# A decoder kernel on one core: expert rows beyond 256 in pieces of 128, and two value products elsewhere

## The chip, the core and the metric

The kernel runs on one NeuronCore of a Trainium2 chip. Its engines have queues of their own and work in order, each: TensorE (PE) multiplies matrices from SBUF into PSUM, VectorE (DVE), ScalarE (ACT) and GpSimd (POOL) work elementwise, SyncE (SP) issues transfers. ACT and POOL issue transfers too; those through a list of row numbers (indirect ones) are issued by POOL. The metric is the device time in microseconds; lower is better. All data is float32, and a float32 matmul stands in the profile as two matmuls and two weight loads.

## The reference, cut to what matters

Two decoder layers follow one another on x, of shape 4 x 512 x 256, each sublayer with a residual and a layer norm. The third one is a mixture of experts: each of the 2048 rows goes to two of 8 experts.

```python
x = layernorm(x + L0_attn(x))               # a recurrence per token
x = layernorm(x + L0_xattn(x, ctx, ctx))    # one head, 1601 context rows
# experts: top 2 of softmax(x @ Wr + br), weights made to sum to 1
h = gelu(xf @ Wi[e] + bi[e]) * sigmoid(xf @ Wg[e] + bg[e])    # 256 -> 1024
r = xf + (h @ Wo[e] + bo[e])
y = (r - mean(r)) * rsqrt(var(r) + 1e-12) * gamma[e] + beta[e]
x = layernorm(x + sum_of_two(weight * y))
x = layernorm(x + L1_attn(x))               # 16 heads, causal
x = layernorm(x + L1_xattn(x, ctx, ctx))    # 16 heads, rotated queries and keys
x = layernorm(x + L1_ffn(x))
```

The number of rows that an expert gets depends on the data, so the kernel must be right for any split of 4096 rows over 8 experts.

## The kernel before, in words

Each stage handles the four batches in turn. In the stages of this study the order of instructions on every engine is the order of the program (`manual_schedule`); waits are put in by the framework, from the tiles that an instruction reads and writes.

**Cross attention of the first layer and routing** (from line 608). For 16 tiles of 128 queries: scores, exponentials, transposed and weighted sums. When a batch is through, the generator `closing` (L719) goes through its tail in steps, one step between the pieces of other work: normalise, transpose x (`to_xT`, L195), then `route` (L457): router logits, softmax, the two largest, ranks by a matmul with a triangular matrix (`before`, `both`), and a row number for each of the row's two places. `scatter` (L528) writes the rows of the batch with 8 indirect transfers into the DRAM array `xs`, 2048 row places per expert. The last batch's tail has no other work beside it. Then `blocks_left` (L539) makes the list of the further blocks.

**Experts** (from line 821). Expert e's first 256 rows are block e. Rows beyond are in further blocks of 256: at most NDYN = 15 of them can be needed, and all 15 are run, so there are 8 + 15 = 23 blocks. Which expert and which rows a further block has stands in `wrow` and `xrow`; its weights and rows come by indirect transfers on POOL's queue, those of the first 8 by plain ones on SP's. The loop (L1007 to L1016) keeps two blocks under way: `begin` loads rows and weights (two buffers for each of eWi, eWg, eWo), `turned` transposes the rows, `first_half` makes the two products with 1024 columns and gelu, sigmoid and their product g, `second_half` the product back to 256, residual, moments, gamma and beta, and stores to the DRAM array `ys`. PE works on block i's first half, then on block i-1's second half. Beside this, the generator `attention_first` (L914) prepares the attention, one step per block.

**Attention of the second layer** (from line 1026). First the sums of the experts' results are gathered back (`combined`, L1069), keys and values of the context are made (`context`, L1173: `key` with a rotation, `value`), then 32 units (batch, group of 4 heads, self or cross) run, the units of cross attention last. The lists `extras` hold work that is put between a unit's pieces; among it are the keys and values of batches 2 and 3 (`later`, L1613), loaded in chunks of the context (`cx`).

Of the kernel before, what the change touches and what calls it, by code (L numbers as in the profile page):

```python
# [17 lines left out]
P = 128  # L18
# [21 lines left out]
def decoder(ctx: ExitStack, tc: tile.TileContext, a: dict, out: bass.AP):  # L40
# [166 lines left out]


    with (
# [55 lines left out]
        xs = tc.dram_tile((ROWS, D), F32, name="xs")  # L265

        def clear_rows():
            zero = p1w.tile([P, 1024], F32, tag="zero", name="zero")
            nc.gpsimd.memset(zero, 0.0)
            zrows = xs.rearrange("(n p r) d -> n p (r d)", p=P, r=4)  # L270
            for i in range(ROWS // (4 * P)):
                nc.sync.dma_start(zrows[i], zero)

# [111 lines left out]
    BLK = 2 * P  # L385
    NDYN = 2 * B * S // BLK - 1
    ys = tc.dram_tile(((E + NDYN) * BLK, D), F32, name="ys")

# [28 lines left out]
    for name, n in (("iota", E), ("base", E), ("more", E - 1), ("upto", E * E), ("dyn", NDYN), ("p", 2)):  # L417
        fields[name] = cmoe[:, at_ : at_ + n]
        at_ += n
# [119 lines left out]
    def blocks_left():  # L539
# [5 lines left out]
        more = prt.tile([P, E, E - 1], F32, tag="more", name="more")  # L545
        nc.vector.tensor_tensor(
            more,
            n[:, :, None].to_broadcast([P, E, E - 1]),
            fields["more"][:, None, :].to_broadcast([P, E, E - 1]),
# [4 lines left out]
        upto = prt.tile([P, E, E], F32, tag="upto", name="upto")  # L554
# [8 lines left out]
        past = prt.tile([P, NDYN, E], F32, tag="past", name="past")  # L563
# [12 lines left out]
        nc.vector.tensor_scalar(j, j, 1.0, float(E - 1), ALU.add, ALU.min)  # L576
# [4 lines left out]
        nc.vector.tensor_scalar(xf, j, float(BLK), None, ALU.mult)  # L581
# [5 lines left out]
        xrow = prt.tile([P, 2, NDYN], I32, tag="xrow", name="xrow")  # L587
        for h in range(2):
            nc.vector.tensor_scalar(xrow[:, h, :], xf, fields["p"][:, h : h + 1], None, ALU.add)
# [6 lines left out]
        nc.vector.tensor_tensor(yf, yf, eks, ALU.subtract)  # L596
# [8 lines left out]
        return wrow, xrow  # L605


    with tc.tile_pool(name="p2", bufs=2) as p2, ExitStack() as ordered:
# [135 lines left out]

        def tail():
            if tails and next(tails[0], tails) is tails:
                tails.pop(0)
# [21 lines left out]
        while tails:  # L769
            tail()  # L770
        ordered.close()
        scatter(B - 1, lambda inst: unordered("xs", inst))
        wrow, xrow = blocks_left()
# [8 lines left out]
    VW = HD + 1  # L782
# [38 lines left out]
    with tc.tile_pool(name="p3", bufs=2) as p3, ExitStack() as ordered:  # L821
# [8 lines left out]
        def begin(i):  # L830

            e = i if i < E else wrow[:, i - E : i - E + 1]
            xb = p3.tile([P, 2, D], F32, tag="xb", name="xb", bufs=3)
            if i < E:
                nc.sync.dma_start(
                    xb, xs[i * B * S : i * B * S + BLK, :].rearrange("(h p) d -> p h d", p=P)
                )
            else:
                for h in range(2):
                    nc.gpsimd.indirect_dma_start(  # L840
                        xb[:, h, :],
                        None,
                        xs,
                        bass.IndirectOffsetOnAxis(ap=xrow[:, h, i - E : i - E + 1], axis=0),
                    )
            wi, wg = expert_first[i] if i < 2 else load_expert(e, expert_in, pmw)
            return i, e, wi, wg, xb

        def turned(i, e, wi, wg, xb):
# [9 lines left out]
            return i, e, wi, wg, xb, xbT  # L859

        def first_half(i, e, wi, wg, xb, xbT):

            (wo,) = load_expert(e, ("eWo",), p3)
            g = p3.tile([P, NF, BLK], F32, tag="g", name="g")
            for w, func in ((wi, AF.Gelu), (wg, AF.Sigmoid)):
                for f0 in range(0, NF, 4):
                    ps = wide()
                    pv = ps.rearrange("p a (h n) -> p (a h) n", n=BLK)
                    dst = g[:, f0 : f0 + 4, :]
                    if w is wg:  # L870
                        dst = p3.tile([P, 4, BLK], F32, tag="sg", name="sg")
                    for k in range(4):
                        f = f0 + k
# [3 lines left out]
                                (w[:, c * FF + f * P : c * FF + (f + 1) * P], xbT[:, c, :])  # L877
# [3 lines left out]
                    for k in range(4):  # L881
                        bias = w[:, 2 * FF + f0 + k : 2 * FF + f0 + k + 1]
                        nc.scalar.activation(dst[:, k, :], pv[:, k, :], func, bias=bias)  # L883
                    if w is wg:
                        part = g[:, f0 : f0 + 4, :]
                        nc.vector.tensor_tensor(part, part, dst, ALU.mult)  # L886

            bo = wo[:, None, NF * D : NF * D + D].to_broadcast([P, 2, D])
            nc.gpsimd.tensor_tensor(xb, xb, bo, ALU.add)
            return i, wo, xb, g  # L890

        def second_half(i, wo, xb, g):
            ps = bank()
            pv = ps.rearrange("p (h d) -> p h d", d=D)
            for h in range(2):
                blk = slice(h * P, (h + 1) * P)
                mm(pv[:, h, :], [(g[:, f, blk], wo[:, f * D : (f + 1) * D]) for f in range(NF)])
            r = p3.tile([P, 2, D], F32, tag="rb", name="rb")
            nc.vector.tensor_tensor(r, pv, xb, ALU.add)
            mv = moments(r, 2)  # L900
            rs = rstd_of(mv, eps12, 2)
            for h in range(2):
                nc.vector.tensor_scalar(
                    r[:, h, :], r[:, h, :], mv[:, h, 0:1], rs[:, h : h + 1], ALU.subtract, ALU.mult
                )
            gam, bet = (
                wo[:, None, (NF + k) * D : (NF + k + 1) * D].to_broadcast([P, 2, D]) for k in (1, 2)
            )
            eng = nc.vector if i == E + NDYN - 1 else nc.gpsimd
# [944 lines left out]
```

## Time and profile before

| | us |
|---|---|
| median of three runs (2436.15 to 2438.79) | 2437.68 |
| the profiled execution | 2439.88 |
| its span | 2438.0 |
| PE busy | 2344.4 |
| DVE busy | 1211.7 |
| ACT busy | 1073.5 |
| POOL busy | 422.7 |
| first matmul of the first expert block | 524.86 |
| end of the last expert block on PE | 1023.1 |
| first self-attention unit ends | 1129.6 |
| cross units | 1488 to 2314 |

A group's line has the program line, the engine, the operation, the tiles (out<-in) with their shapes, the count, and behind the bar the busy time, the mean length of one in ns, and the idle time of the engine just before, with what ended it. Matmuls overlap one another, so the mean length is more than their spacing. In a timeline a line has start, length, and the idle time before it in brackets. L202 is the helper `mm`, through which most matmuls go: the tiles tell them apart.

### The profile page before, as it was taken

Reading aid. Unit: us, or ns where it says so; the run is one execution under the profiler, and the core shown is the slowest. Engines: PE = TensorE matmul, PEld = TensorE weight load, DVE = VectorE, ACT = ScalarE, POOL = GpSimd, SP = SyncE. Lnnn points to the kernel's source line nnn. Section 1 sums busy time; section 2 is a strip of 40 time slices with the busy share of each in tenths; the row PEclk is TensorE's granted clock in tenths of the full one; section 3 lists DMA queues with packets and bytes.
Section 4 is the critical chain, followed back from the end, with each engine's and each line's share of the span. In section 5 each row is a group of like instructions: output and inputs, shape, how many; then the busy total and the mean of one; then the engine's idle time right before and its main releaser. Section 6 shows DMA issues by size and latency. Waiting matters only on the chain.

```text
span 2438.0 us, 34867 instructions
## 1 busy us (share of the span) xinstructions
PE 2344.4 (96%) x13928; PEld 1328.2 (54%) x13928; DVE 1211.7 (50%) x2854; ACT 1073.5 (44%) x1996; POOL 422.7 (17%) x429
## 2 busy tenths in 40 slices
PE   7898999959999999989999999999999999999998
PEld 4767677748888888843333334333333333333256
DVE  1333334322222233266656667666666666677334
ACT  1111122114444544424555453655666566566730
POOL 1010001121144433345130010222110010000000
PEclk9999999969999999989999997999999999999999
DMA  8300311145667555351211210112110110100100
GB/s 307 150 1 3 124 54 45 49 143 186 247 239 266 198 204 201 124 164 50 66 48 35 95 36 5 39 51 60 51 37 16 45 36 16 30 34 18 31 9 26
DMA packets 76112, 215.84 MB, mean 89 GB/s; under 512 B 11816, under 2 KB 35630, under 8 KB 66862
## 3 DMA queue, kind: packets, MB, share of 16 engines
q1 hardware_dynamic: 61790, 133.04, 16.1%
q0 software_dynamic: 10992, 65.54, 7.3%
q10 hardware_dynamic: 3168, 15.03, 1.8%
q8 instruction: 110, 1.80, 0.3%
q14 instruction: 52, 0.43, 0.1%
HBM read 171.53 MB, written 53.21 MB: 92 GB/s over the span
## 4 chain that ended last, share of the span: by engine, by line
PE 51%; ACT 1%; DVE 1%; issue 0%; DVEq 0%; ACTq 0%
PE s L1310 23%; PE one L202 12%; PE po L1337 11%; PE s L202 2%; PE s L1320 1%; PE one L1295 1%; PE one L1358 1%; ACT x L171 0%; ACT ex L1324 0%; DVE one L1269 0%; PE one L1379 0%; PE one L1477 0%; PE one L1400 0%; DVE pm L1267 0%; DVE st L156 0%
## 5 line engine op out<-in xcount | busy, mean ns | idle before, releaser
L1324 ACT ACTIVATE ex<-s 128x512 f32<-128x512 f32 (+1 forms) x1062 | 577.9, 594 | 466.9 <-PE s L1310 236.7
L1267 DVE TENSOR_REDUCE pm<-one 128x1 f32<-128x512 f32 x768 | 493.7, 685 | 174.5 <-PE s L1310 123.3
L1310 PE MATMUL s<-q,kc 32*128 32x512 f32 x1612 | 524.1, 640 | 0.2 <-ACT ex L1324 0.2
L202 PE MATMUL one<-kc,qt 32*128 32x512 f32 (+1 forms) x2048 | 483.8, 564 | 0.3 <-DVE pm L1267 0.3
L1310 PEld LDWEIGHTS s<-q,kc 32*128 32x128 f32 x1612 | 161.6, 179 | 210.9 <-issue 175.5
L1337 PE MATMUL po<-ex,v 128*32 128x256 f32 (+3 forms) x2472 | 245.1, 465 | 0.3 <-ACT ot L1350 0.3
L1269 DVE CUSTOM_DVE_ANT_0 one<-one,c_diagq 128x512 f32<-128x512 f32 x256 | 171.9, 716 | 75.6 <-PE one L202 63.5
L1310 PE MATMUL s<-q,ks 32*128 32x512 f32 x512 | 179.8, 650 | 5.3 <-ACT ex L1324 4.9
L1337 PEld LDWEIGHTS po<-ex,v 128*32 128x32 f32 (+1 forms) x2472 | 49.8, 108 | 232.2 <-issue 225.5
L886 DVE TENSOR_TENSOR g<-g,sg 128x1024 f32<-128x1024 f32 x46 | 57.2, 1243 | 235.8 <-ACT sg L883 235.7
L202 PE MATMUL wide<-xbT,eWi 128*128 128x256 f32 x736 | 168.9, 389 | 4.0 <-DVE xbT L858 4.0
L202 PEld LDWEIGHTS one<-kc,qt 32*128 32x128 f32 x2048 | 164.2, 188 | 11.6 <-DVE pm L1267 7.9
L202 PE MATMUL wide<-xbT,eWg 128*128 128x256 f32 x736 | 162.6, 379 | 0.0
L202 PE MATMUL bank<-eWo,g 128*128 128x256 f32 x736 | 162.5, 379 | 0.0
L202 PEld LDWEIGHTS wide<-xbT,eWi 128*128 128x128 f32 x736 | 143.5, 196 | 25.8 <-issue 4.2
L202 PE MATMUL one<-ks,qt 32*128 32x512 f32 x512 | 152.6, 665 | 3.7 <-ACT raw L1182 2.7
L202 PEld LDWEIGHTS wide<-xbT,eWg 128*128 128x128 f32 x736 | 139.7, 190 | 19.2 <-ACT g L883 0.2
L1150 POOL TENSOR_TENSOR raw<-raw,c_cos 128x512 f32<-128x512 f32 (+1 forms) x32 | 34.9, 1092 | 660.5 <-DVE swp L1149 578.1
L202 PEld LDWEIGHTS bank<-eWo,g 128*128 128x128 f32 x736 | 138.2, 190 | 17.9
L883 ACT ACTIVATE g<-wide,eWi 128x256 f32<-128x256 f32 x184 | 71.7, 476 | 72.3 <-PE wide L202 69.7
L1310 PEld LDWEIGHTS s<-q,ks 32*128 32x128 f32 x512 | 53.8, 185 | 83.4 <-issue 62.0
L202 PE MATMUL wide<-ctxT,q 128*128 128x512 f32 (+1 forms) x256 | 91.3, 510 | 0.8 <-DVE q L649 0.8
(319 smaller groups left out, 2988.4 us busy)
## 6 DMA issues: line engine op xcount, KB each, us to landing
xs<-zero SPq DMA_DIRECT2D x32, 512.0 KB
kc<-kcd SPq DMA_DIRECT2D x16, 800.5 KB
eWo<-in_eWo SPq DMA_DIRECT2D x8, 1408.0 KB
cx<-in_ctxT SPq DMA_DIRECT2D x18, 512.0 KB
eWi<-in_eWi SPq DMA_DIRECT2D x8, 1028.0 KB
eWg<-in_eWg SPq DMA_DIRECT2D x8, 1028.0 KB
qt<-qd SPq DMA_DIRECT2D x32, 256.0 KB
ctxT<-in_ctxT SPq DMA_DIRECT2D x4, 1601.0 KB
```

The source lines that it names most:

```text
L202: nc.tensor.matmul(ps, l, r, start=(i == 0), stop=(i == n - 1))
L883: nc.scalar.activation(dst[:, k, :], pv[:, k, :], func, bias=bias)
L886: nc.vector.tensor_tensor(part, part, dst, ALU.mult)
L1150: eng.tensor_tensor(raw[:, :n], raw[:, :n], cos[:, :n], ALU.mult)
L1267: nc.vector.tensor_reduce(pm[:, t, j, c : c + 1], ps, AX.X, ALU.max)
L1269: nc.vector.tensor_tensor_reduce(out=ps, in0=ps, in1=diagq[:, 384 - t * P : 896 - t * P], scale=1.0, scalar=LOWEST, op0=ALU.add, op1=ALU.m ...
L1295: nc.tensor.transpose(pt[:, t * P : (t + 1) * P], ng.rearrange("p j r -> p (j r)"), ident)
L1310: nc.tensor.matmul(ps[:kn], kt[rows, k * P : k * P + kn], q2[rows, :], start=True, stop=cross)
L1320: nc.tensor.matmul(ps[:, k * P : (k + 1) * P], later_[:, :P], later_[:, P:], start=False, stop=True)
L1324: nc.scalar.activation(ex[:kn, h, :], ps[:kn], AF.Exp)
L1337: nc.tensor.matmul(state["po"][j * 32 : j * 32 + 32, q0:q1], (vals if cross else vself)[b % 2][:kn, k, c0 : c0 + 32], ex[:kn, j % 2, q0:q1 ...
L1358: nc.tensor.transpose(pt[:, t * P : (t + 1) * P], ot[:, t * P : (t + 1) * P], ident)
```

## The change

The further rows of an expert go in pieces of 128 rows instead of blocks of 256. A block takes two pieces, each with its own expert, so a block of pieces needs two sets of weights, and its first products have 128 columns instead of 256. At most NDYN = 28 pieces can be needed, 14 blocks. Eleven of them run always, mixed with the 8 first ones in the order `ffmfmfmmfmfmmfmfmmm` (f a first block, m one of pieces); each of the last three runs only if the list is that long, inside nested `tc.If` on a count that every engine loads into a register. Parts of `ys` that those three would write are cleared at the start. Weights are now loaded name by name and piece by piece, right after the piece of the running block that frees the buffer; the bias of the second product moves from POOL's addition on xb to a DVE addition on r, and moments and normalisation of a block of pieces are made for each half.

The values of batches 2 and 3 for the second layer's cross attention are made in the tail of the routing of the last batch: four ahead of its transposes, twelve ahead of the ranks' matmul, ten after `blocks_left`; they go to the DRAM arrays `vd` and are loaded back in one transfer each in the cross units of batches 1 and 2. DVE clears and sets the rest of these tiles. `blocks_left` now stands ahead of the last scatter.

In the start of the attention, the rotation of every second chunk of keys goes from DVE to POOL, the order of the work is changed, and the load of the exponential table stands later.

```diff
@@ clear_rows
+            for n in range(22, NDYN, 2):
+                row = E * BLK + n * P
+                nc.sync.dma_start(
+                    ys[row : row + 2 * P, :].rearrange("(p r) d -> p (r d)", r=2), zero[:, : 2 * D]
+                )
...
+        def rows_of_values():
+            big = p2in.tile([P, NT * S2], F32, tag="fs", name="v23")
+            rest = p2in.tile([P, KHALF * D], F32, tag="ctxa", name="v2")
...
+            for b_ in (2, 3):
+                nc.vector.memset(places[b_, NKT - 1], 0.0)
+            for t in (big[:, : 22 * VROW], rest[:, : 4 * VROW]):
+                t = t.rearrange("p (k r) -> p k r", r=VROW)
+                nc.vector.memset(t[:, :, NH * VW :], 0.0)
+                heads = t[:, :, : NH * VW].rearrange("p k (h r) -> p k h r", r=VW)
+                nc.vector.memset(heads[:, :, :, HD : HD + 1], 1.0)
+
+        def value(b, k):
+            kn = kn_of(k)
+            ps = bank()[:, :D]
+            mm(ps[:kn], [(ctxTs[b][:, c, k * P : k * P + kn], xaV[:, c, :]) for c in range(2)])
+            dst = places[b, k][:kn, : NH * VW].rearrange("p (h r) -> p h r", r=VW)
+            nc.scalar.copy(dst[:, :, :HD], ps[:kn].rearrange("p (h r) -> p h r", r=HD))
...
-        while tails:
-            tail()
+        values = [lambda b=b, k=k: value(b, k) for b in (2, 3) for k in range(NKT)]
+        for n in (0, 4, 0, 0, 0, 12, 0, 0, 0, 0, 0):
+            if n == 4:
+                tail()
+                rows_of_values()
+            else:
+                tail()
+            for f in values[:n]:
+                f()
+            values = values[n:]
+        assert not tails
+        wrow, xrow, count = blocks_left()
+        for f in values:
+            f()
         ordered.close()
         scatter(B - 1, lambda inst: unordered("xs", inst))
-        wrow, xrow = blocks_left()
...
+        def halves(kind, m):
+            return (m,) if kind == "first" else (2 * m, 2 * m + 1)
+
+        def weights_of(block, name, h):
+            kind, m = block
+            hs = halves(*block)
+            if h < len(hs):
+                e = m if kind == "first" else wrow[:, hs[h] : hs[h] + 1]
+                loaded.setdefault((block, name), []).extend(
+                    load_expert(e, (name,), p3 if name == "eWo" else pmw)
+                )
...
+        def first_half(block, nxt):
+            xbT = loaded.pop((block, "xT"))
             g = p3.tile([P, NF, BLK], F32, tag="g", name="g")
+            for name, func in (("eWi", AF.Gelu), ("eWg", AF.Sigmoid)):
+                ws = loaded.pop((block, name))
+                for i in range(2):
+                    if len(ws) == 1:
+                        w, fs_, cols = ws[0], range(4 * i, 4 * i + 4), slice(0, BLK)
+                    else:
+                        w, fs_, cols = ws[i], range(NF), slice(i * P, (i + 1) * P)
...
+                    if nxt and (nxt, name) not in first_loads:
+                        weights_of(nxt, name, i)
...
+        def second_half(block, nxt, after):
...
             for h in range(2):
+                wo = wos[h % len(wos)]
                 blk = slice(h * P, (h + 1) * P)
                 mm(pv[:, h, :], [(g[:, f, blk], wo[:, f * D : (f + 1) * D]) for f in range(NF)])
+                if len(wos) == 1 and h == 0:
+                    continue
+                hs = slice(0 if len(wos) == 1 else h, h + 1)
+                k = hs.stop - hs.start
+                nc.vector.tensor_tensor(r[:, hs], pv[:, hs], xb[:, hs], ALU.add)
...
+                nc.vector.tensor_tensor(r[:, hs], r[:, hs], bo, ALU.add)
...
+                eng = nc.gpsimd if nxt else nc.vector
+                eng.tensor_tensor(r[:, hs], r[:, hs], gam, ALU.mult)
+                eng.tensor_tensor(r[:, hs], r[:, hs], bet, ALU.add)
...
+                for half in range(2) if len(wos) == 1 else (h,):
+                    if nxt:
+                        weights_of(nxt, "eWo", half)
+            if after:
+                rows_of(after)
...
+        def run(blocks, work):
+            get = lambda i: blocks[i] if i < len(blocks) else None
+            for b in blocks[:2]:
+                rows_of(b)
+            for name in ("eWi", "eWg", "eWo"):
+                for h in range(2):
+                    if (blocks[0], name) not in first_loads:
+                        weights_of(blocks[0], name, h)
+            turned(blocks[0])
+            for i, b in enumerate(blocks):
+                first_half(b, get(i + 1))
+                if get(i + 1):
+                    turned(get(i + 1))
+                if i:
+                    second_half(blocks[i - 1], b, get(i + 2))
+                elif get(2):
+                    rows_of(get(2))
+                next(work, None)
+            second_half(blocks[-1], None, None)
+
+        order = "ffmfmfmmfmfmmfmfmm" + "m" * 1
...
+        def beside():
+            ready["total"] = nc.values_load(count[0:1, 0:1], min_val=0, max_val=NDYN)
+            yield from attention_first()
...
+        def rest(m):
+            if m < NDYN // 2:
+                with tc.If(ready["total"] > 2 * m):
+                    with tc.manual_schedule():
+                        run([("more", m)], iter(()))
+                    rest(m + 1)
+        rest(11)
...
-                eng = nc.gpsimd if here is None else nc.vector
+                eng = nc.gpsimd if here is None or i % 2 else nc.vector
...
-        for f in keys0[0:2] + values1 + add + keys0[4:6] + turn:
+        for f in keys0[0:2] + values1[:8] + add + values1[8:] + turn + keys0[4:6]:
...
-        later = [
-            context(2, range(4), ()) + context(3, range(2), ()),
-            context(3, range(2, 4), ()) + context(2, (), range(4)),
-            context(3, (), range(4)),
-        ]
+        later = [context(2, range(4), ()), context(3, range(4), ())]
+        for b in (2, 3):
+            starts[index[b - 1, 1, True]].append(
+                lambda b=b: nc.sync.dma_start(vals[b % 2].rearrange("p k r -> p (k r)"), vd[b])
+            )
```

## The prediction

> **What bounds the kernel now.** I read the page's slices first, then the groups, then the timeline of single engines at the two borders of the expert stage.
>
> ```profile
> span 2438.0 us, 34867 instructions
> PE 2344.4 (96%) x13928; PEld 1328.2 (54%) x13928; DVE 1211.7 (50%) x2854; ACT 1073.5 (44%) x1996; POOL 422.7 (17%) x429
> ...
> PE   7898999959999999989999999999999999999998
> ...
> DMA  8300311145667555351211210112110110100100
> ...
> L202 PE MATMUL wide<-xbT,eWi 128*128 128x256 f32 x736 | 168.9, 389 | 4.0 <-DVE xbT L858 4.0
> ```
>
> A slice is 61 us. TensorE (PE) has one hole, the slice that begins at 488 us (digit 5), where the routing of the last batch ends. The expert blocks follow (to 1023 us, PE full, DMA at 5 to 7 tenths), then the attention, again PE. The span is 2438.0, the profiled run 2439.88, the median of runs 2437.68: what lies round the span is 2 us, so I carry differences of the span straight to the median.
>
> In the timelines, a line gives start, length, instructions, and the idle time before it:
>
> ```profile
> 59.35 1.06 PE L202 MATMUL bank<-inv,dg 128*128 128x128 f32 x8
> ...
> 490.37 2.30 PE L188 MATMUL wide<-ident,x 128*128 128x128 f32 x8 [3.19 <-DVE x L726]
> ...
> 505.49 0.64 PE L202 MATMUL bank<-both,before 128*128 128x32 f32 x2 [5.75 <-DVE both L492]
> ...
> 522.99 1.09 PE L854 MATMUL bank<-ident,xb 128*128 128x128 f32 x4 [15.80 <-DMA xb<-xs]
> 524.86 10.09 PE L202 MATMUL wide<-xbT,eWi 128*128 128x256 f32 x32 [0.78 <-DVE xbT L858]
> ...
> 753.12 7.07 PE L202 MATMUL bank<-eWo,g 128*128 128x256 f32 x32
> ...
> 1024.00 7.14 PE L202 MATMUL one<-xaV,qt 128*128 128x256 f32 x32 [0.93 <-DVE rb L899]
> ```
>
> Spacing of matmuls: 32 of 256 columns take 7.07, the last of them 0.38, so (7.07-0.38)/31 = 0.216 us each. Eight of 128 columns take 1.06, the last 0.28: 0.112 each. So half the columns cost half, although each needs new weights. A block now is 96 x 0.216 + 4 transposes x 0.11 = 21.2 us, and the stores of the blocks do stand 21.2 apart. The weights' transfers are hidden:
>
> ```profile
> 747.54 0.95 POOL L397 DMA_INDIRECT eWi<-in_eWi,wrow  x1 [0.30 <-issue]
> ...
> 760.71 1.27 POOL L889 TENSOR_TENSOR xb<-xb,eWo 128x512 f32<-128x512 f32 x1 [9.70 <-DMA eWo<-in_eWo,wrow]
> ```
>
> Three transfers (3.55 MB) land 13.2 us after the first issue, in a period of 21.2.
>
> **The change, part by part.**
>
> *Blocks.* 23 blocks become 19: 8 first ones, 11 of two pieces. The last three run only for a list over 22 pieces. From the reference on its inputs I counted the rows per expert: 520, 304, 1112, 352, 989, 298, 70, 451. Beyond 256 that is 3+1+7+1+6+1+0+2 = 21 pieces, so they don't run. A block of pieces: 128 matmuls x 0.112 + 32 x 0.216 + 0.44 = 21.7. Stage: 23 x 21.2 = 487 now; 8 x 21.2 + 11 x 21.7 = 408 then: -79.
>
> Two things give back. (a) The two halves of the second product lie in one PSUM bank, and by the order of instructions the second half's first matmul now waits for the VectorE (DVE) addition of the first half. That addition stands on DVE behind the last product g (1.23) and the copy xbT (0.68), and g behind ScalarE's (ACT) last sigmoid, some 2.6 us after PE's last matmul of the first half (8 of 128 columns, 0.32 each, estimated from 1.57 for four of 256 and 1.09 for two of 512). So the addition ends near 14.3+2.8+1.2+0.7+0.4 = 19.4 in the block, PE could go on at 18.2: about 1.3 us when the block running is one of pieces (5 times with the end), 0.7 when it is a first block (6 times): +11. (b) Traffic: a block of pieces loads 7.1 MB, with rows and results 7.6. At the full rate seen (273 GB/s at a DMA share of 0.75, so 364) that is 20.9 us, under the 23 of such a block; at the pace of the lines above (3.55 MB in 13.2, latency and all) 28. Several transfers stand queued at once here, so I take the nearer first one and +4 for four places where blocks of pieces meet; ends 0 and +55. All eight indirect transfers of a block go through POOL's queue, 1.26 us each, 10 us, with 3 us of gamma and beta: under 23. Each weight load waits in that queue for PE and ACT to free its buffer; behind it stand gamma, beta and the row gathers, of which the rows have least room, some 2 us. SP's queue has the same waits for first blocks, with the ys stores behind them. The bias addition that moves from POOL to DVE (0.69) is hidden: DVE is a quarter busy. Blocks: -64.
>
> *Values of batches 2 and 3.* 26 products of 4 matmuls leave the attention. There PE is 100% busy between 1977 and 2286 us, so their time counts: 104 x 0.216 = -22.5. From one copy of the attention's sums (ACT L1350) to the next, the first three cross units of batch 2, with 40 of these matmuls, last 160.3 in all and those of batch 3, with none, 149.8; less two query projections of 1.7 that is 0.18 each, -18; the group's busy time (40.1/144 = 0.28) gives -29. I take -23. The 10 us of ACT copies were hidden; the two loads of 1.9 MB on SP's queue run at a DMA share of 0.1.
>
> They go into the hole, which is not wholly free, for the chain there passes through PE's queue. Four stand ahead of the transposes (L188), and two PSUM buffers force the third to wait for an ACT copy, which waits for new DVE memsets (about 1.9 us, six of 60 to 350 columns at the pace of the row 0.69 for 512), which wait for normalising. Transposes then start near 495.5 instead of 490.4: +5. Twelve stand ahead of "both": 48 x 0.216 = 10.4, some cold, against 5.75 idle: +6. Routing ends 11 later, then come the unchanged 8 scatters and the row load. The last ten values run under those. I give back 1 for a warmer clock: +10, ends +3 and +16.
>
> *The clock rule.* The line at 524.86 is the row: after 15.8 idle, 32 matmuls took 10.09, not 7.07: 3.0 lost. The Trainium skill (TensorE: Matmul & The Clock Gate, Part 1) says PE halves its clock after an idle window of 3.4 us and needs about as long busy to get it back, which would make 1.7 lost per hole. By the row a hole costs 3.0. This speaks against the new stop at the branch.
>
> *The branch.* Today PE idles 0.93 between stages. Now PE's first matmul after the join waits for DVE and ACT to have passed the branch, so DVE's whole tail shows. The last block's tail today is 1023.16 to 1027.61, 4.45 us, at 512 columns; at 256, with one addition more and the output bias after it, 4. Then compare, semaphores and branch: 0.5 to 1. The Trainium skill (Runtime: NRT & Kernel Launch, Instruction fetch mechanics) says that a taken branch to code outside the prefetched pages stops the engine for a fetch. The trace has no branch; a 16 KB instruction packet takes 0.94 in it. By that rule up to two fetches on the slowest engine, an estimated 2.6 each (0.94, and the 1.65 from a weight transfer's issue to its first packet); without, 0. The three skipped blocks are short (44 instructions on ACT, 25 on DVE each), so I take 1. With 4+1+1-0.9 and 3.0 cold: +8, ends +3 and +18. Later things (gathers of ys, cx loads) wait as long, and shift with it. The register loads of the count, a form not in the trace: the same page has about 0.2 us for one and 1.3 for several, so 0 to 1.5, taken 0.5 on PE.
>
> *Order after the stage.* Rotations of chunks 1 and 3 go from DVE to POOL; 0.69 x 3 becomes 1.27 x 3, behind the gathers of batch 1, which hold POOL to about 50 us after the stage. DVE gains 7 us where PE idles 2.73 and 0.98: -2, ends -6 and +4. The moved table load (1.28) is hidden on ACT. Zeroing 0.75 MB of ys more is hidden in a slice with DMA 0 to 3.
>
> **Sum.** -64 -23 +10 +8 +0.5 -2 = -70.5: 2437.7 - 70.5 = 2367 us.
>
> **Rivals.**
> 1. Likeliest, as above: 2367, own range 2345 to 2388. Chance 0.62.
> 2. DMA becomes the bound in part: each block of pieces lasts 27 us, not 23: 11 x 4 = +44: 2411. For it: 13.2 us per 3.55 MB from POOL; against it 273 GB/s without a full queue. Chance 0.16.
> 3. The hole is freer and the values dearer than I take: hole +3, values -29, branch +4: 2350, and no DMA loss: 2346. For it: PE idles 30 us there. Chance 0.14.
> 4. Slower: the indirect transfers of two experts at a time don't reach the rate. The gain of 70 is gone when a block of pieces lasts 23 + 70/11 = 29.4, that is 7.6 MB at 259 GB/s; at 245 it is 31 and the kernel 2455. The pace of the lines above, 269, is close to it. Chance 0.07.
> That the skipped blocks run (21 pieces against a bound of 22) or that nothing changes I give 0.01.
>
> **Numbers.** Runs of this kernel tell 0.2% (5 us) from no change. Ends: case 3 with the order after the stage at -6 and the branch at +3 gives 2341, so 2340 below; case 2 in full gives 2411, cut to 2405, since what lies above 2405 (half of case 2, case 4) and below 2340 should hold 2 in 10. Faster 0.92 (cases 1 to 3), same 0.01, slower 0.07.
>
> **What would show it.** Right: matmuls of 128 columns spaced 0.112; ys stores of blocks of pieces 22 to 24 apart; a PE wait of the second eWo half on DVE L991; PE idle of 5 to 8 ahead of the first xaV matmul after the branch; first block starting near 533; units of cross 1 and 2 two to four us shorter. Wrong: PE waits on DMA eWo, eWi or xb of many us in the blocks, PE clock below 1.0 there, or a POOL queue held by a buffer not yet free.

## The result, and the profile after

| | before | changed kernel |
|---|---|---|
| median | 2437.14 us | 2429.2 us (2422.99 to 2432.43) |
| ratio of the changed kernel to before, 95% interval | 1 | 0.9967 (0.9956 to 0.9977) |
| the profiled execution, its span | 2439.88, 2438.0 | 2425.35, 2423.5 |

The change gains 8 us where 70 were forecast; 2429 lies outside the range of 2345 to 2388. A second comparison on another chip, further down, gives 0.9985, with an interval that reaches 1.

The page of the changed kernel, with the same rows as before (slices of 61 us, then the groups):

```profile
span 2423.5 us, 36202 instructions
PE 2289.2 (94%) x14448; PEld 1296.1 (53%) x14448; DVE 1197.9 (49%) x2846; ACT 1063.4 (44%) x2103; POOL 435.3 (18%) x455
...
PE   7898999979898999789999999999999999999998
...
DMA  8300211145788767432210220111120010100100
...
L202 PE MATMUL bank<-eWo,g 128*128 128x256 f32 x608 | 151.9, 410 | 17.1 <-DMA eWo<-in_eWo,wrow 11.3
```

PE lost 55 us of work, but its share of the span fell from 96% to 94%: holes came in. Those in the expert blocks are seen in the slices that begin at 606, 727 and 970 us, with 8, 8 and 7 where PE had 9 before (the last of them also covers the border to the next stage). Over the blocks PE's mean granted clock went from 0.99 to 0.95. The DMA row there was at 5 to 7 tenths and is at 6 to 8.

To see how much each stretch gave, I cut both profiled executions at five marks: on PE the first expert matmul, the start of the last eWo matmul and the first xaV matmul of the next stage; on ACT the copies of the sums (ot<-po) that end the first unit and the last.

| stretch, us | before | after | difference | forecast |
|---|---|---|---|---|
| to the first expert matmul | 524.9 | 531.2 | +6.3 | +10 |
| expert blocks | 497.8 | 477.0 | -20.8 | -64 |
| border to the next stage | 1.3 | 8.0 | +6.7 | +8 (with cold PE) |
| from there to the first unit | 105.6 | 115.2 | +9.6 | -2 |
| the units | 1184.2 | 1167.9 | -16.3 | -23 |

The sum is -14.5, the difference of the two spans. Some 5 of it are chance: the router's matmuls of the batch before the last, which the change doesn't touch, began at 456.19 in this execution and at 461.24 in that of before. From there to the first expert matmul it is 63.6 before and 75.0 after: the values cost +11.4 there. Without that chance the sum is -9, near the medians.

The routing of the last batch, in the timeline of PE:

```profile
488.55 3.52 PE L202 MATMUL bank<-xaV,ctxT 128*128 128x256 f32 x8 [4.68 <-ACT v L789]
...
499.18 13.65 PE L202 MATMUL bank<-xaV,ctxT 128*128 128x256 f32 x48
512.66 0.30 PE L202 MATMUL bank<-both,before 128*128 128x32 f32 x2
...
529.34 1.09 PE L933 MATMUL bank<-ident,xb 128*128 128x128 f32 x4 [6.60 <-DMA xb<-xs]
531.21 9.54 PE L202 MATMUL wide<-xbT,eWi 128*128 128x256 f32 x32 [0.78 <-DVE xbT L937]
```

Both stops that the forecast named are there: the wait for an ACT copy of a value, and 48 matmuls that `both` waits behind.

The expert blocks show what was not forecast. First the PE waits of the stage (in total, times, longest), then a first block and what follows it in the timeline of PE:

```profile
PE bank L933 <- DMA xb<-xs,xrow: 24.0, 7, 5.8
PE bank L202 <- DMA eWo<-in_eWo,wrow: 11.3, 4, 6.9
...
PE bank L202 <- DVE rb L991: 5.2, 9, 0.6
```

```profile
595.61 7.07 PE L202 MATMUL wide<-xbT,eWi 128*128 128x256 f32 x32
602.51 7.07 PE L202 MATMUL wide<-xbT,eWg 128*128 128x256 f32 x32
615.43 1.14 PE L933 MATMUL bank<-ident,xb 128*128 128x128 f32 x4 [5.84 <-DMA xb<-xs,xrow]
616.36 6.10 PE L202 MATMUL bank<-eWo,g 128*128 128x256 f32 x16
623.03 3.72 PE L202 MATMUL bank<-eWo,g 128*128 128x256 f32 x16 [0.57 <-DVE rb L991]
626.59 7.31 PE L202 MATMUL wide<-xbT,eWi 128*128 128x128 f32 x64
```

The matmuls themselves cost what was forecast: 64 of 128 columns take 7.31, (7.31-0.28)/63 = 0.112 each. The wait of the second eWo half on DVE is 0.57. But PE stands 5.84 for rows, and the 16 matmuls after it take 6.10 where 16 take 3.62. Seven such slow eWo groups in the stage, those that follow a hole, lose 14.6 us together, beside the 35 of the waits themselves.

Why the rows are late is seen on POOL, in the same stretch:

```profile
577.86 1.27 POOL L1005 TENSOR_TENSOR rb<-rb,eWo 128x512 f32<-128x512 f32 x1
579.07 0.40 POOL L1024 CAST later<-c_later 128x256 bf16<-128x256 f32 x1
599.61 1.27 POOL L1004 TENSOR_TENSOR rb<-rb,eWo 128x512 f32<-128x512 f32 x1 [20.15 <-DVE rb L999]
600.96 1.26 POOL L1005 TENSOR_TENSOR rb<-rb,eWo 128x512 f32<-128x512 f32 x1
602.37 0.99 POOL L407 DMA_INDIRECT eWo<-in_eWo,wrow  x1
603.67 0.96 POOL L407 DMA_INDIRECT eWo<-in_eWo,wrow  x1 [0.31 <-issue]
604.93 0.96 POOL L922 DMA_INDIRECT xb<-xs,xrow  x1 [0.30 <-issue]
606.20 0.96 POOL L922 DMA_INDIRECT xb<-xs,xrow  x1 [0.30 <-issue]
607.47 0.95 POOL L407 DMA_INDIRECT eWi<-in_eWi,wrow  x1 [0.30 <-DMA turn<-in_c_cos]
```

The gamma multiplication (L1004) stands at the head of POOL's queue for 20 us, waiting for DVE to normalise the block before. Eight loads are queued behind it (the fence ends with the fifth) and then go out one after another. Over the stage, POOL's waits at this line come to (in total, times, longest):

```profile
POOL rb L1004 <- DVE rb L999: 227.6, 26, 21.3
```

A queue that stands is not new. The kernel before had this between 680 and 1030 us:

```profile
POOL xb L889 <- DMA eWo<-in_eWo,wrow: 139.4, 15, 10.6
```

There it cost little, and PE was busy for 494.8 of the stage's 498 us: each round's five transfers had been issued ahead of the addition that waited (L889). The change put the arithmetic ahead of the loads. The windows of 5 us show what this does to the transfers (columns: length; busy time and count of PE, its weight loads, DVE, ACT and POOL; PE's granted clock; DMA share; GB/s):

```profile
595.00:600.00 5.00, 5.00 (x25) 4.41 (x24) 3.25 (x9) 0.29 (x1) 0.39 (x1) 1.00 0.13 27
600.00:605.00 5.00, 5.00 (x25) 4.41 (x24) 0.00 (x0) 2.97 (x6) 4.16 (x5) 1.00 1.04 340
605.00:610.00 5.00, 4.58 (x22) 3.69 (x20) 0.74 (x1) 4.51 (x10) 3.78 (x5) 1.00 0.97 356
610.00:615.00 5.00, 0.00 (x0) 0.00 (x0) 1.71 (x2) 2.54 (x5) 3.03 (x2) 0.96 1.00 415
615.00:620.00 5.00, 4.57 (x13) 3.80 (x14) 0.69 (x1) 0.00 (x0) 0.00 (x0) 0.50 0.99 416
```

The DMA engines are nearly idle from 595 to 600 and full from 600 to 620. Over the whole stage they move 273 GB/s, at a share of 0.73. The clock of 0.50 after the hole is the cold PE.

At the border, PE again:

```profile
1008.55 1.02 PE L202 MATMUL bank<-xaO,bv 128*1 128x256 f32 x4
1012.55 0.69 PE L202 MATMUL bank<-xa_bo,ones 1*128 1x256 f32 x2 [2.97 <-DVE xa_bo L1096]
1016.24 9.36 PE L202 MATMUL one<-xaV,qt 128*128 128x256 f32 x32 [3.00 <-PEq L1146]
...
1062.56 2.07 PE L202 MATMUL one<-qkvV,xT 128*128 128x256 f32 x4 [6.79 <-ACT raw L1256]
1066.41 2.07 PE L202 MATMUL one<-qkvV,xT 128*128 128x256 f32 x4 [1.78 <-ACT raw L1256]
```

The output bias (xaO,bv and xa_bo) now comes after the last block: `attention_first` goes one step per block, and four blocks fewer leave its last two steps over. Then PE's own queue waits 3.00 for the branch. At 1062 and 1066 PE waits 8.6 for ACT, which waits for free `raw` tiles. In the trace ACT's wait ends when a rotated tile has been stored (kcd<-raw), and POOL, behind its gathers, begins the first rotation only at 1053.79. ACT, then POOL:

```profile
1061.90 0.60 ACT L1256 ACTIVATE raw<-one 128x512 f32<-128x512 f32 x1 [10.57 <-DMA kcd<-raw]
```

```profile
1053.79 1.27 POOL L1282 TENSOR_TENSOR raw<-raw,xT 128x512 f32<-128x512 f32 x1
```

### The profile page after: what moved, and what is told of

Its sections match the earlier page's. It is cut to its first block, busy times and chain, and to the rows that moved or that the text cites. A ratio compares the mean times of both kernels' runs of the same rounds, so it can differ in the third digit from the quotient of the medians.

```text
span 2423.5 us, 36202 instructions
## 1 busy us (share of the span) xinstructions
PE 2289.2 (94%) x14448; PEld 1296.1 (53%) x14448; DVE 1197.9 (49%) x2846; ACT 1063.4 (44%) x2103; POOL 435.3 (18%) x455
## 4 chain that ended last, share of the span: by engine, by line
PE 50%; DVE 1%; ACT 1%; issue 0%; DVEq 0%; ACTq 0%
PE s L1442 23%; PE po L1469 12%; PE one L202 11%; PE s L202 2%; PE s L1452 1%; PE one L1427 1%; PE one L1490 1%; ACT x L171 0%; ACT ex L1456 0%; DVE pm L1399 0%; DVE one L1401 0%; PE one L1511 0%; PE one L1609 0%; PE one L1532 0%; DVE nb L166 0%
## 5 line engine op out<-in xcount | busy, mean ns | idle before, releaser
L1442 PE MATMUL s<-q,kc 32*128 32x512 f32 x1612 | 529.9, 640 | 0.9 <-ACT ex L1456 0.8
L1469 PE MATMUL po<-ex,v 128*32 128x256 f32 (+3 forms) x2688 | 252.2, 444 | 0.3 <-ACT ot L1482 0.3
L202 PE MATMUL bank<-eWo,g 128*128 128x256 f32 x608 | 151.9, 410 | 17.1 <-DMA eWo<-in_eWo,wrow 11.3
L202 PEld LDWEIGHTS bank<-eWo,g 128*128 128x128 f32 x608 | 123.7, 208 | 40.4 <-issue 10.7
L971 DVE TENSOR_TENSOR g<-g,sg 128x1024 f32<-128x1024 f32 x38 | 46.5, 1224 | 196.4 <-ACT sg L969 177.1
L202 PE MATMUL wide<-xbT,eWi 128*128 128x128 f32 (+1 forms) x960 | 139.5, 306 | 4.0 <-DVE xbT L937 4.0
L202 PEld LDWEIGHTS wide<-xbT,eWi 128*128 128x128 f32 x960 | 130.5, 193 | 12.3 <-issue 3.4
L202 PE MATMUL wide<-xbT,eWg 128*128 128x128 f32 (+1 forms) x960 | 137.0, 303 | 0.0
L202 PEld LDWEIGHTS wide<-xbT,eWg 128*128 128x128 f32 x960 | 128.1, 191 | 6.6
L98 ACT ACTIVATE sd<-mv,eps 128x1 f32<-128x1 f32 (+2 forms) x34 | 10.0, 295 | 188.9 <-DVE mv L109 188.8
```

The source lines that it names most:

```text
L98: nc.scalar.activation(sd, mv[:, :, 1], AF.Sqrt, bias=eps)
L202: nc.tensor.matmul(ps, l, r, start=(i == 0), stop=(i == n - 1))
L1442: nc.tensor.matmul(ps[:kn], kt[rows, k * P : k * P + kn], q2[rows, :], start=True, stop=cross)
L1469: nc.tensor.matmul(state["po"][j * 32 : j * 32 + 32, q0:q1], (vals if cross else vself)[b % 2][:kn, k, c0 : c0 + 32], ex[:kn, j % 2, q0:q1 ...
```

## The experiments

All runs stand in one table; their edits and what they told follow. The ratio is to the kernel before, with its 95% interval; the stretches are those of the table above.

| run | median us | ratio | start | blocks | border | to unit | units |
|---|---|---|---|---|---|---|---|
| changed kernel again | 2429.1 | 0.9985 (0.9966 to 1.0004) | 536.4 | 482.2 | 8.0 | 114.5 | 1167.7 |
| rows earlier | 2390.1 | 0.9812 (0.9795 to 0.9830) | 535.8 | 446.4 | 8.4 | 112.3 | 1167.6 |
| gamma, beta on DVE | 2402.3 | 0.9869 (0.9854 to 0.9883) | 535.0 | 452.2 | 8.0 | 116.6 | 1164.6 |
| both of these | 2389.6 | 0.9815 (0.9792 to 0.9839) | 536.7 | 439.5 | 8.0 | 115.2 | 1171.7 |
| rotations on DVE | 2421.9 | 0.9954 (0.9937 to 0.9971) | 536.4 | 477.7 | 8.4 | 105.2 | 1170.4 |
| no branch | 2429.6 | 0.9983 (0.9971 to 0.9995) | 536.5 | 475.5 | 6.1 | 115.1 | 1168.5 |
| values left in the attention | 2435.5 | 1.0006 (0.9994 to 1.0018) | 522.6 | 478.6 | 8.5 | 114.9 | 1184.8 |
| steps paired | 2441.8 | 1.0034 (1.0015 to 1.0054) | 533.3 | 489.3 | 4.1 | 119.4 | 1170.8 |
| rows, rotations, steps paired | 2398.0 | 0.9845 (0.9828 to 0.9862) | 535.0 | 458.7 | 4.1 | 110.3 | 1165.7 |
| the same, weights earlier | 2392.3 | 0.9830 (0.9817 to 0.9843) | 536.1 | 453.2 | 4.1 | 108.5 | 1165.7 |
| gamma and beta, rows, rotations | 2380.9 | 0.9779 (0.9757 to 0.9801) | 534.8 | 438.8 | 8.4 | 106.3 | 1167.0 |
| the same on another chip | 2385.1 | 0.9789 (0.9769 to 0.9810) | 536.0 | 439.4 | 8.1 | 105.6 | 1170.4 |
| the same, weights earlier, steps paired | 2384.5 | 0.9800 (0.9779 to 0.9820) | 536.8 | 440.9 | 4.3 | 110.9 | 1166.0 |
| three causes and the old order | 2377.4 | 0.9757 (0.9737 to 0.9778) | 534.0 | 439.3 | 8.5 | 101.7 | 1170.4 |
| the same, no branch | 2377.7 | 0.9757 (0.9737 to 0.9777) | 531.5 | 438.4 | 5.6 | 101.1 | 1170.3 |

**Rows a block earlier.** A fourth xb buffer lets the rows be asked for ahead of the block instead of behind the gamma, beta and eWo of the block before. Three small tiles (c_later, ones16, dia) share the place of two others to make room.

```diff
-            xb = p3.tile([P, 2, D], F32, tag="xb", name="xb", bufs=3)
+            xb = p3.tile([P, 2, D], F32, tag="xb", name="xb", bufs=4)
...
-            for b in blocks[:2]:
+            for b in blocks[:3]:
                 rows_of(b)
...
             for i, b in enumerate(blocks):
+                if i and get(i + 2):
+                    rows_of(get(i + 2))
                 first_half(b, get(i + 1))
...
-                    second_half(blocks[i - 1], b, get(i + 2))
-                elif get(2):
-                    rows_of(get(2))
+                    second_half(blocks[i - 1], b, None)
```

> The rows of each block are asked for one block earlier (a fourth xb buffer); bytes, matmuls and every other load stay. Theory A, the row gathers stand too late on POOL's queue, behind gamma, beta and the eWo loads, and each hole that this leaves costs a cold stretch besides: the PE waits on xb<-xs,xrow fall from 24.0 us to under 3, six groups of 16 eWo matmuls that took 4.8 to 6.1 us go back to 3.7 (about 9 us), and some 5 us return as waits on eWo: about 2429 - 28 = 2401 us, 0.985 of the kernel before (0.981 to 0.990). Theory B, the transfers' rate is the limit (7.6 MB a block of pieces): the same bytes are late all the same, the waits move from xb to eWo and eWi: 2424 to 2430 us, 0.995 to 0.997.

2390.1 us, 0.9812: theory A, at the strong end of what it gave. With the same bytes the stage became 30.6 us shorter than in the first trace of the changed kernel (446.4 against 477.0; 482.2 in the second). The waits of PE:

```profile
PE bank L202 <- DMA eWo<-in_eWo,wrow: 12.5, 5, 6.8
PE bank L933 <- DMA xb<-xs: 6.5, 1, 6.5
PE bank L202 <- DVE rb L991: 5.3, 9, 0.7
```

The line of xb<-xs,xrow is gone; that of eWo, 11.3 before, is 12.5. The 6.5 on xb<-xs is the load ahead of the first block, outside the stage. So the rate of the transfers was not the limit. Nor were the waits on POOL as such: L1004 still waits for DVE 26 times, 184.9 us in all (between 536 and 975), but the rows no longer stand behind it.

**Gamma and beta on DVE.**

```diff
-                eng = nc.gpsimd if nxt else nc.vector
+                eng = nc.vector
```

> The changed kernel with gamma and beta of every block on DVE, so that POOL's queue holds no arithmetic in the expert stage. Theory A1, the loads are late because eWo's two buffers hold one block of pieces only and come free when the block before has used gamma and beta, with the rows queued behind them: who computes gamma and beta matters little, the PE waits on xb<-xs,xrow stay above 15 us, the time within 6 us of the changed kernel. Theory A2, the arithmetic on POOL is itself what delays the loads (2.5 us a block): the xb waits fall below 8 us and the time by 15 to 25 us.

2402.3 us, 0.9869, 27 us less than the changed kernel beside it; the waits on xb<-xs,xrow fell from 24.7 to 6.2. That is what A2 expected (a little over its 15 to 25), though not for its reason: the arithmetic is 2.5 us a block, and the gain is in what its wait held. POOL in the same place as above:

```profile
582.45 0.96 POOL L407 DMA_INDIRECT eWo<-in_eWo,wrow  x1 [9.23 <-issue]
612.51 0.94 POOL L407 DMA_INDIRECT eWo<-in_eWo,wrow  x1 [29.11 <-DMA xT<-in_c_sin]
613.76 0.95 POOL L922 DMA_INDIRECT xb<-xs,xrow  x1 [0.30 <-issue]
```

The next block's first eWo now goes out at 582, not at 602, since one of eWo's two buffers was free all along; only the second has to wait. A1 was wrong in taking the buffers for the cause of all of it. The second eWo waits 29.11; the profile names a transfer as what ended it, but the addition of beta (L1005, on DVE now), after which the buffer is free, ended at 611.74, just before. So the queue still stands, with the rows behind it, but the burst is one load shorter.

At the place shown this gains nothing. The rows go out later than in the changed kernel (78.8 us after the stage's first matmul, not 73.7), an earlier plain row load is now waited for 5.99, and the next block begins 95.8 us after the stage's first matmul, where it was 95.4. The gain comes at later places: at the next one the rows go out at nearly the same time (125.5, not 126.4) but land after 6.8 us instead of 8.3, and PE waits 0.23 instead of 3.64. That the shorter burst is what makes them land earlier fits this, but no run tests it alone.

**Both together.**

> Gamma and beta on DVE and the rows a block earlier, together. Gamma and beta alone gave 0.987, the rows alone 0.981. If both remove the same thing (a POOL queue that stands for 20 us and then issues everything at once), the gains do not add: 0.979 to 0.981. If they remove different waits (rows: xb; gamma and beta: eWo and xb of first blocks), the xb waits are gone and of the eWo waits only the last block's 6 to 7 us is left: some 8 us better than the rows alone, 0.976 to 0.978. If the additions were full: 0.970.

0.9815, as the rows alone. The first of the three holds by the medians: the gains do not add, both remove the same late loads. (POOL's queue still stands in this run; its eWo loads wait 72.9 us in three times for L1005.) In the stage itself 7 us more went (446.4 to 439.5), and some 7 came back behind it.

**Rotations of batch 0 on DVE.**

```diff
-                eng = nc.gpsimd if here is None or i % 2 else nc.vector
+                eng = nc.gpsimd if here is None else nc.vector
```

> All rotations of the keys of batch 0 go back to DVE (in the changed kernel those of chunks 1 and 3 are on POOL). Theory D, those rotations stand on POOL behind the gathers of batch 1, keep raw tiles in use and make ACT and then PE wait (8.6 us of PE waits on ACT raw): 2429 - 8 = 2421 us, 0.993 of the kernel before. Rival: the 9.6 us lost between the first xaV matmul and the first unit come from the branch (gathers and loads that start later) and a cold PE: within 2 us of the changed kernel, 0.996 to 0.997.

0.9954, beside 0.9983 for the run without the branch on the same chip: 7.7 us by their medians, with intervals that meet at 0.9971; against the changed kernel's own two ratios it is 3 and 8 us. The stretch to the first unit went from 115 to 105.2, and the 8.6 us of waits on ACT raw are gone. Theory D holds. The same edit on top of the two others took 8.7 us by the medians, 0.9815 to 0.9779 with intervals that overlap:

> As the run before it, and the rotations of batch 0 all on DVE: 8 us less than that run (10 gained before the first unit, 2 given back in the units): 0.973 to 0.975. If the rotations' gain was chance of one trace: the same as that run.

**No branch.** `rest(11)` is taken out; its blocks are not needed for this list.

> The three conditional blocks and their branch are left out (this list needs 11 blocks of pieces, so the output stays whole). Theory C, the branch costs what stands at the border (6.7 us more idle before the first xaV matmul, 2.2 more in the matmuls after it): 2429 - 9 = 2420 us, 0.993 of the kernel before. Rival: the engines only wait there for work that is late anyway (cx loads, gathers of ys), and the time comes back some microseconds later: 2426 to 2430, 0.9955 to 0.997.

0.9983: the rival. In the trace PE's wait on its own queue is gone and the border shrank by 1.9 us; the wait of 2.97 for the output bias and the cold matmuls (9.36 again) stayed.

**Values left in the attention.** `values = []` in the routing, no tiles and loads of `vd`, and the list `later` as before.

> The values of batches 2 and 3 go back into the attention, the blocks stay as changed. By the two traces the values' move cost 6.4 us before the first expert matmul and took 16.4 from the attention: without it 2429 - 6 + 16 = 2439 us, 1.001 of the kernel before. By the forecast's terms (+10 and -23): 2442, 1.002. Rival: the later start is not due to the values but to longer routing arithmetic or the loads beside it: the first expert matmul stays near 531 and the time is 2445, 1.003.

1.0006, so moving the values is worth 5 to 10 us, by which of the two comparisons of the changed kernel one takes. In the trace the first expert matmul comes at 522.6 again and the units take 1184.8: from the router's matmul on it is 63.3 where the changed kernel has 75.0, 11.7 less, and 16.9 more in the units. Theory and measurement agree; the rival is out.

**Steps paired.** Two steps of `attention_first` beside each of three blocks, so that the output bias falls into the stage.

```diff
                 next(work, None)
+                if i in (4, 6, 8):
+                    next(work, None)
```

> The changed kernel with three early steps of the work beside the blocks paired (the ones that only start row transfers), so that the output bias is made inside the expert stage. If the bias at the border (1.02 + 2.97 + 0.69 us) is on the path: 4 to 5 us below the changed kernel, 0.9955 of the kernel before. If the first products of the next stage are bound by the tables, gathers and copies behind the border anyway: within 2 us of the changed kernel, 0.997 to 0.998, with the gap at the border some 4 us shorter and the stretch to the first unit as much longer.

1.0034, 12 to 16 us slower than the changed kernel by its two ratios, which neither theory had. The border shrank by 3.9 us and the stretch to the unit grew by 4.9: what the second expected. The stage grew by 7 besides. The waits on plain row loads (xb<-xs) are 22.5 us there against 11.4 in the second trace of the changed kernel; which transfers hold them up is not shown. An earlier form of the pairing, beside blocks 4, 8 and 12, is in these two runs:

> Rows a block earlier, the rotations of batch 0 all on DVE, and three more steps of the work beside the blocks, so that the output bias (xaO,bv and xa_bo,ones) is made inside the stage and not after it. If the causes add: 0.981 from the first, 8 to 10 us from the rotations, 4.7 us (1.02 + 2.97 + 0.69) from the bias: 0.976 of the kernel before (0.973 to 0.979). If the border is set by the branch and not by the bias, its 8 us stay and the ratio is 0.978; if the rotations' 10 us come back in the units after them, 0.980.

> As the run with three causes removed, and besides, where a block of pieces follows a first block, the first piece's eWi and eWg are asked for a block earlier, ahead of gamma and beta on POOL, into the buffer that is free then. If what is left of the loss is the burst of six weight loads after gamma and beta (eWo waits of 1 to 2 us in five places), it falls by 3 to 8 us against that run: 0.973 to 0.975. If the eWo loads are late because their own buffers come free late, which this leaves as it is, nothing changes: within 2 us of it.

Both miss their numbers: 0.9845 and 0.9830, behind the rows alone. There, two steps that read the mask fell into one block, and DVE waited for the second one's transfer with g, the copy xbT and the next addition behind it (DVE, then PE):

```profile
854.51 0.36 DVE L1070 TENSOR_SCALAR mf<-mi 16x398 f32<-16x398 int32 x1 [7.33 <-DMA mi<-in_mask]
...
855.39 2.34 DVE L971 TENSOR_TENSOR g<-g,sg 128x1024 f32<-128x1024 f32 x2
...
858.25 0.40 DVE L991 TENSOR_TENSOR rb<-bank,xb 128x256 f32<-128x256 f32 x1
```

```profile
858.71 6.43 PE L202 MATMUL bank<-eWo,g 128*128 128x256 f32 x16 [6.36 <-DVE rb L991]
```

Asking for weights a block earlier (the second of the two) gave 5.5 us in the stage and 5.8 by the medians, with intervals that overlap. On top of gamma and beta, with the pairing beside blocks 4, 6 and 8, nothing was left to gain:

> As the run before it, and the first piece's eWi and eWg asked for a block earlier where a block of pieces follows a first block, and the steps beside the blocks paired as in the first run of this call. Early weights can take away what is left of the waits on eWo and eWi inside the stage (about 3 us), the pairing at most 4: 0.971 to 0.974. If neither is on the path any more: the same as the run before it.

0.9800, behind the run it was built on (0.9779), not measurably.

**The changed kernel again.**

> The changed kernel itself, as the reference for the three runs beside it: 0.995 to 0.998 of the kernel before.

0.9985, with an interval that meets the first one's. Its stage was 482.2.

**The old order of items.** What was still open: the stretch between the blocks and the first unit, with the rotations back on DVE, still had a wait of 4.58 us, in PE's and then ACT's timeline:

```profile
1014.17 1.97 PE L202 MATMUL one<-xaV,cx 128*65 128x256 f32 x4 [4.58 <-ACT v L1323]
```

```profile
1005.60 0.37 ACT L1323 COPY v<-one 128x256 f32<-128x256 f32 x1 [0.49 <-PE one L202]
1010.66 0.30 ACT L125 ACTIVATE sd<-mv,eps 128x4 f32<-128x4 f32 x1 [4.69 <-DVE mv L161]
...
1011.78 2.07 ACT L171 ACTIVATE x<-x,nb,rstd 128x256 f32<-128x256 f32 x4 [0.59 <-DVE nb L166]
1013.76 1.16 ACT L1323 COPY v<-one 128x256 f32<-128x256 f32 x4
```

ACT waits for the moments of batch 0's sums, which the changed order puts ahead of the last five copies of values, and PE runs out of PSUM buffers.

```diff
-        for f in keys0[0:2] + values1[:8] + add + values1[8:] + turn + keys0[4:6]:
+        for f in keys0[0:2] + values1 + add + keys0[4:6] + turn:
```

> The kernel with three causes removed (gamma and beta on DVE, rows a block earlier, rotations of batch 0 on DVE) once more, as the reference for the two runs beside it: 0.976 to 0.980 of the kernel before.

> As the reference run, with the items after the stage in the order of the kernel before (all values of batch 1, then the sums of batch 0, then keys, then the transposes). In the changed order the sums' normalising stands on ACT ahead of the last five copies of values, and PE waits 4.6 us for a PSUM buffer there. If that order is what is left of the loss before the first unit: 4 to 6 us below the reference run, the stretch from the first xaV matmul to the first unit near 101 instead of 106. If the sums are late because ys and its gathers are late, the wait only moves to the transposes: within 2 us of the reference run.

> As the run before it, and without the three conditional blocks and their branch (this list needs 11 blocks of pieces, the output stays whole). If the engines' stop at the branch is still paid (3.4 us of PE's wait on its queue there): 2 to 4 us less than that run. If the bias at the border and the tables behind it cover the branch: within 1.5 us of it.

The reference repeats at 0.9789. With the old order the stretch to the first unit is 101.7, as the first theory had it, and the median falls by 7.7 us, more than the 4 to 6 expected and with intervals that just overlap, to 2377.4 us: 0.9757, the best of all these kernels. Taking out the branch as well changes nothing by the medians, though the border is 2.9 us shorter in the trace. So by the medians the branch costs nothing, by the trace at most those 3 us; the intervals, 5 us to each side, can't tell these apart. The conditional blocks may stay.

## Why the prediction was wrong

The forecast was -70.5 in all, the result -8 (-3.6 in the second comparison). The steps, with what the runs showed:

- **Blocks, part (b), traffic and POOL's queue: the step that failed.** I put +4, with an upper end of 55, and wrote that gamma, beta and row gathers stand behind the loads and that "the rows have least room, some 2 us". Then I only added up POOL's busy time (10 + 3 us under 23) and went on as if a queue with time to spare were a queue in time. L1004's wait on DVE came to 227.6 us over 26 instructions in the stage, the longest 21.3, and all loads behind it wait as long. What counts is which loads those are: with the rows ahead of it, the same line still waited 184.9 us, and the stage was 30.6 us shorter. The signs that I had named for being wrong are in the trace: PE waits on xb and eWo, a clock below 1.0, and a POOL queue that is held, though by arithmetic and not by a buffer. The stage's blocks became 20.8 us (15.6 in the second trace) shorter, not 64: the missing 43 are 35 of waits on xb<-xs,xrow and eWo and 14.6 of cold matmuls, less the 4 that I had counted and the 6 by which the PSUM wait came out smaller, 40 in all. That this is the cause is shown: with the rows earlier and gamma and beta off POOL the blocks last 438.4 to 439.5 in five traces, which is 58 to 59 less than before, close to the -64. What is left in the best kernel is two holes, both on eWo loads, of 4.5 and 6.7 us, with 2.7 and 2.8 of slower matmuls behind them.
- **Rivals 2 and 4, transfers as the limit, are wrong in their cause.** They enclose the time (2411, and 2437 and more), but the same bytes moved at 296 GB/s over the stage of the best kernel, at a share of 0.78, against 273 in the changed one. It was the order of issue, not the rate.
- **Matmuls (-79): right.** 0.112 each, as forecast.
- **PSUM wait (+11): right in kind, too large.** 0.57 each, nine times, 5.2 in all, where I had 1.3 and 0.7; my sum also put 2.8 for ACT's delay where the text before it had 2.6.
- **Start (+10): right.** +11.4 from the router's matmul on.
- **Values (-23): too large.** The units gave 16.3, in the run without that part 16.9. The keys of batch 3 that moved into the units of batch 1 with the new list `later` were no part of my sum, but they only move work within the units. I had 0.18 and 0.28 a matmul as ends and took 0.216; 104 matmuls gave 0.16 each, below the lower end.
- **Branch (+8): right in size, wrong in cause.** The border grew by 6.7 and the cold matmuls after it by 2.2 (9.36 against 7.14). But without the branch the border is only 2 to 3 us shorter, and no time is gained by the medians. Whether a fetch of instructions has a part in these, no run shows; nor does one separate the register loads (+0.5). The other part, the output bias left over by a loop with four iterations fewer, I had counted in its DVE tail; moving it into the stage only moved the wait, as the runs with paired steps showed.
- **Order after the stage (-2, ends -6 and +4): wrong.** It was +9.6, of which 2.2 are the cold matmuls. I wrote that DVE gains where PE idles; what I left out is that the rotated tile is freed later on POOL, behind the gathers that I had named myself. Rotations back: -10 in that stretch; the old order, on top: -4.
- **The cold clock.** The row that I took, 3.0 us lost in a hole of 15.8, was good for the largest hole in the blocks (3.0 after 6.9 us); the holes ahead of the other six slow groups, of 1.9 to 5.8 us, lost 1.2 to 2.5. I had set it at one place, the branch, and not at the holes that a late load leaves.

By the table: blocks 43 short, the stretch behind them some 10, values 7, the start 1. That is 61 of the 62 missing.

## What to carry to other kernels

In an engine's queue that issues transfers, an instruction that waits for another engine makes everything behind it wait as long, and a sum of busy times doesn't show it. Before moving a load in such a queue, write down what stands ahead of it and when that instruction's own input is ready; if an engine with time to spare can take the arithmetic, or one more buffer lets the load go ahead of it, the load that is needed first is no longer late, even where the queue still stands for others. When a loop loses iterations, look at what was spread over them, and what a moved step waits for.

## What the hardware showed besides

A hole need not be long to slow PE down. After one of 1.90 us, 16 eWo matmuls took 5.38 us, 1.8 more than the usual 3.62 (a granted clock of 0.66 in the window from 835 to 840). After one of 2.11 us in the same trace 16 took 3.69, and so they did in the run with earlier rows after one of 1.90. Which of the two happens, no run here tells. The rule that the prediction weighed (the Trainium skill, TensorE: Matmul & The Clock Gate, Part 1: an idle window of 3.4 us), by which a hole would cost an estimated 1.7, is near in size: the runs show 1.2 after a hole of 3.64 us and 3.0 after one of 6.91. But it doesn't give the loss after a hole shorter than its window.

At a DMA share of about 1.0 the windows shown move 340 to 416 GB/s, where the stage's mean before was 208 at 0.56. The rate at full share that I had worked out, 364 from a mean rate and a mean share, lies in the middle of a wide span.

Three nested conditional blocks that are not taken showed 2.5 to 3.5 us of PE's wait on its own queue. Without them the border was 1.9 and 2.9 us shorter, and the medians did not move (2429.6 beside 2429.1 and 2429.2; 2377.7 beside 2377.4).
